# Three-layer graph convolution on one core: an opening whose edges come as one block a partition and are turned round by TensorE, and 16.5 instead of 15 chunks a dense block in layer 1

## The chip, the core and the metric

One core of a Trainium2 chip runs the whole program as one launch. The metric is the device time of one execution in microseconds (us); lower is better. TensorE (PE, with its weight loads as PEld), VectorE (DVE), ScalarE (ACT), GpSimd (POOL) and SyncE (SP) each run their own instructions in program order, and wait for each other by semaphores. DMAs are issued from the queues of SP, ACT and POOL.

## The reference, cut to what matters

```python
# x: (6250, 256) f32; src, dst: 100000 edges, sorted by dst
# W1: (256, 512), W2: (512, 512), W3: (512, 256)
def _gcn_layer(h_in, W, b, src, dst, norm_edge, n_nodes):
    h = h_in @ W
    msg = h[src] * norm_edge[:, None]
    agg = jax.ops.segment_sum(msg, dst, num_segments=n_nodes)
    return agg + b
src = jnp.concatenate([edge_index[0], loops])
dst = jnp.concatenate([edge_index[1], loops])
deg = jax.ops.segment_sum(jnp.ones_like(dst, dtype=x.dtype), dst, num_segments=n)
dinv = jnp.where(deg > 0, jax.lax.rsqrt(deg), 0.0)
norm_edge = dinv[src] * dinv[dst]
h = x
for W, b in ((W1, b1), (W2, b2), (W3, b3)):
    h = jax.nn.relu(_gcn_layer(h, W, b, src, dst, norm_edge, n))
# the kernel's result: _layernorm(x + h, axis=-1)
```

## The kernel before, in words

The 6250 nodes are cut into NB = 50 blocks of Q = 125 nodes; five groups of GRP = 10 blocks share an opening stage. Because the edges are sorted by their target, a block's edges are one run. Of each run the first CAP = 2048 edges are held as KF = 16 chunks of 128, and what lies behind them goes to a shared "rest" of each group. A layer sums neighbours in one of two ways. For a **gathered** block, each chunk is one indirect DMA from GpSimd (line 1260) that fetches 128 rows of a table in device memory, and one or two matmuls with a 0/1 matrix of the targets (line 1290) that add them into the block's 125 rows. For a **dense** block, the count matrix of the block against all 6250 nodes (`counts`, comparisons at line 603, matmuls at 678, copies at 637) is multiplied with all rows held on chip (`parts`): 50 matmuls of 512 columns (line 1362). In layer 1 the first FEW = 22 blocks are dense and the other 28 gathered; both kinds run interleaved, chunk by chunk, in an order written out by the Python loop in `layer`.

How many dense products a chunk gets stands in three lines, `first` being 10 and `spacing` 15 in layer 1 (called with i = 0), `done` the products so far and `begun` 0:

```python
until = min(len(dense) * NB, begun + int((chunk + 1 - first) * NB / spacing))
if i == 0:
    until = min(until, done + 3)
```

The part ahead of layer 1 is called the opening here. `tile_gnn_resnorm_kernel` first finds where each block's run begins (`at`, `line`, and `starts` for the DMA registers). Then `sorted_path` does this, in an order written out by hand:

- `load_edges` issues one DMA a block, 50 in all: 128 partitions with 16 edges each, that is runs of 128 bytes. SP issues 25 of them, ACT 15 and GpSimd 10 (line 712). They fill `ed`.
- `load_x` brings the rows of x for each group, two DMAs a group (`by_rows` cuts 125 rows into 112 and 13). Groups 0 and 1 are issued by GpSimd at the very start, groups 2, 3 and 4 by GpSimd behind its edges. `rows_of(room, g)` places groups 0 to 3 in the four quarters of `room`; group 4 has `last_x`.
- `counted(g)` has three stages for each group. The first takes the targets relative to the block (`dlo`, `near`, lines 779 and 782), and has TensorE and ScalarE find where they rise (784, 786, 788, 791). The second counts the degrees (796 to 806), in group 0 after `rest_counted`. The third takes 1/sqrt (808), scales the group's ten blocks of x in place (ACT at line 814, from group 2 on every second block on DVE at line 812) and stores them to the table `tab` in two halves of five blocks (line 79 of `by_rows`, on SP). In step k of the loop stand stage one of group k, stage three of group k-2 and stage two of group k-1.
- `upper(g)` (ACT, 822) and `lower(g)` (DVE, 826) split the scaled rows into the two halves of `parts`.
- `searches` finds the runs that the count matrices are made from (503 to 563), `matrices` makes these, two sub-matrices a step. Before, three of its steps stand in step k = 5 of the loop and two in k = 6.

The first gather of layer 1 waits for the last store to `tab`. `both_stored` then stores `parts` to a second table, five blocks at a time, from chunk 2 on every 5 chunks; `other_parts` splits group 3 in the first chunks.

## Time and profile before

| | |
|---|---|
| median of 3 runs | 2048.05 us (2047.35 to 2074.66) |
| profiled execution, its own time | 2061.76 us |
| span in its profile, first to last instruction | 2060.0 us |
| mean granted TensorE clock | 0.98 |
| PE / PEld busy | 1930.2 us (94%) / 1508.0 us (73%) |
| DVE / ACT / POOL busy | 1538.2 / 1330.5 / 1436.8 us |

The rows come from one profiled execution. Times in a row are microseconds from the start of its span unless marked ns; a row of a timeline is `start, duration, engine, line, operation, out<-in, count, [idle before <- what ended it]`. An engine name with a q behind it (SPq, ACTq) is the queue that issues DMAs.

### The profile page before, as it was taken

Reading aid. Unit: us, or ns where it says so; the run is one execution under the profiler, and the core shown is the slowest. Engines: PE = TensorE matmul, PEld = TensorE weight load, DVE = VectorE, ACT = ScalarE, POOL = GpSimd, SP = SyncE. Lnnn points to the kernel's source line nnn. Section 1 sums busy time; section 2 is a strip of 40 time slices with the busy share of each in tenths; the row PEclk is TensorE's granted clock in tenths of the full one; section 3 lists DMA queues with packets and bytes.
Section 4 is the critical chain, followed back from the end, with each engine's and each line's share of the span. In section 5 each row is a group of like instructions: output and inputs, shape, how many; then the busy total and the mean of one; then the engine's idle time right before and its main releaser. Section 6 shows DMA issues by size and latency. Waiting matters only on the chain.

```text
span 2060.0 us, 30151 instructions
## 1 busy us (share of the span) xinstructions
PE 1930.2 (94%) x8561; PEld 1508.0 (73%) x8561; DVE 1538.2 (75%) x2881; ACT 1330.5 (65%) x2525; POOL 1436.8 (70%) x1436
## 2 busy tenths in 40 slices
PE   4499999999997989999999999999999899999997
PEld 3377777777774657888777778888878778787785
DVE  5866787778776658877677886689778477777777
ACT  3566777677775657766567766677756565665553
POOL 4366766766767577777777777677776577777773
PEclk9999999999998999999999999999999999999998
DMA  8796989999999798998599988989989467777772
GB/s 174 256 289 187 253 242 248 250 255 253 259 246 323 208 290 255 276 285 267 171 270 276 265 235 261 278 262 260 271 251 252 118 182 189 187 187 193 180 190 81
DMA packets 228116, 482.83 MB, mean 234 GB/s; under 512 B 45117, under 2 KB 83583, under 8 KB 227940
## 3 DMA queue, kind: packets, MB, share of 16 engines
q0 software_dynamic: 123136, 315.59, 55.5%
q1 hardware_dynamic: 102500, 164.99, 28.0%
q8 instruction: 69, 1.13, 0.2%
q14 instruction: 107, 0.88, 0.1%
q10 hardware_dynamic: 2304, 0.25, 0.1%
HBM read 412.41 MB, written 68.25 MB: 233 GB/s over the span
## 4 chain that ended last, share of the span: by engine, by line
PE 74%; DMA 13%; issue 5%; POOL 3%; DVE 3%; ACT 1%; SPq 1%; POOLq 0%; ACTq 0%; DVEq 0%
PE sacc L1290 16%; PE smm L1362 7%; PE sacc L1362 7%; PE win_ps L1362 6%; PE mat_ps L1362 6%; DMA room<-tab,ssrc 6%; PE win_ps L1499 5%; DMA parts<-tab,ssrc 2%; PE win_ps L1519 2%; PE str L1362 2%; PE near_cols L1030 2%; PE str L1499 2%; PE sacc L1030 2%; PE mat_ps L1030 2%; PE smm L1030 2%
## 5 line engine op out<-in xcount | busy, mean ns | idle before, releaser
L1260 POOL DMA_INDIRECT room<-tab,ssrc x714 | 732.3, 1026 | 239.4 <-issue 105.5
L1290 PE MATMUL sacc<-halves,shot 128*125 128x512 f32 (+1 forms) x1596 | 558.8, 412 | 23.4 <-DVE halves L1326 6.8
L1326 DVE TENSOR_TENSOR halves<-room,halves 128x256 fp32r<-128x256 f32 (+1 forms) x641 | 339.8, 543 | 155.9 <-ACT halves L1322 147.6
L1260 POOL DMA_INDIRECT halves<-both,ssrc x352 | 333.8, 948 | 144.3 <-issue 35.7
L1322 ACT CAST halves<-room 128x256 fp32r<-128x256 f32 (+1 forms) x641 | 306.2, 501 | 153.9 <-DMA room<-tab,ssrc 116.6
L1198 ACT CAST piece<-room 125x625 fp32r<-125x625 uint8 x423 | 299.5, 716 | 126.8 <-PE mat_ps L1362 42.7
L1290 PEld LDWEIGHTS sacc<-halves,shot 128*125 128x125 f32 x1596 | 294.6, 189 | 116.0 <-DVE halves L1326 20.4
L603 DVE TENSOR_TENSOR room<-near_cols,slots 128x625 bf16<-128x625 f32 (+2 forms) x387 | 293.1, 804 | 56.3 <-PE sacc L678 22.5
L1260 POOL DMA_INDIRECT parts<-tab,ssrc x246 | 270.5, 1099 | 83.9 <-issue 50.6
L1362 PE MATMUL sacc<-parts,piece 125*125 125x512 f32 x600 | 192.9, 428 | 0.4 <-ACT piece L1198 0.4
L1362 PE MATMUL smm<-parts,piece 125*125 125x512 f32 x655 | 187.0, 405 | 0.6 <-DVE piece L1198 0.6
L1326 DVE TENSOR_TENSOR halves<-parts,halves 128x512 fp32r<-128x512 f32 x185 | 126.1, 695 | 53.0 <-ACT halves L1322 49.7
L1362 PE MATMUL win_ps<-parts,piece 125*125 125x512 f32 x550 | 152.3, 403 | 4.8 <-ACT piece L1198 4.8
L1362 PE MATMUL mat_ps<-parts,piece 125*125 125x512 f32 x550 | 150.1, 397 | 0.0
L678 PEld LDWEIGHTS <-room 128*125 128x125 bf16 x650 | 90.2, 141 | 71.8 <-issue 34.1
L1185 DVE TENSOR_TENSOR shot<-near_cols,sdlo 128x500 fp32r<-128x500 f32 x191 | 128.2, 671 | 18.9 <-PE sacc L1290 13.9
L1322 ACT CAST halves<-parts 128x512 fp32r<-128x512 f32 x185 | 111.8, 620 | 45.3 <-DMA parts<-tab,ssrc 17.4
L1362 PEld LDWEIGHTS smm<-parts,piece 125*125 125x125 f32 x655 | 117.8, 186 | 30.0 <-issue 3.5
L1499 PE MATMUL win_ps<-room,w_sb 128*128 128x250 f32 x512 | 123.6, 385 | 10.4 <-ACT room L1478 9.6
L1362 PEld LDWEIGHTS win_ps<-parts,piece 125*125 125x125 f32 x550 | 102.8, 190 | 30.5 <-ACT piece L1198 5.2
L976 DVE TENSOR_TENSOR parts<-parts 125x512 fp32r<-125x512 f32 x150 | 103.7, 692 | 25.3 <-ACT parts L974 24.0
L1499 PEld LDWEIGHTS win_ps<-room,w_sb 128*128 128x128 f32 x512 | 98.9, 195 | 28.4 <-ACT room L1478 12.4
(349 smaller groups left out, 3606.8 us busy)
## 6 DMA issues: line engine op xcount, KB each, us to landing
parts<-tab SPq DMA_DIRECT2D x166, 224.0 KB
kept<-room SPq DMA_DIRECT2D x30, 683.6 KB
room<-kept SPq DMA_DIRECT2D x30, 683.6 KB
tab<-st SPq DMA_DIRECT2D x74, 224.0 KB
room<-tab,ssrc POOLq DMA_INDIRECT x714
both<-parts SPq DMA_DIRECT2D x10, 1120.0 KB
own_row<-tab SPq DMA_DIRECT2D x38, 224.0 KB
parts<-kept SPq DMA_DIRECT2D x60, 136.7 KB
```

What stands on the lines that cost most here:

```text
L603: nc.vector.tensor_tensor(out, (keys if near_taken else near_cols)[:, :shape[2]].unsqueeze(1).to_broadcast(shape), numbers.unsqueeze(2).to ...
L678: nc.tensor.matmul(bank[:Q, len(pair) * 256:][:, :G * NB], lhsT=hot_lo, rhs=hot_key, start=True, stop=True)
L976: nc.vector.tensor_sub(to[:, HID:], row, to[:, :HID].bitcast(F32))
L1030: nc.tensor.matmul(team_banks[n][:, :TEAM * Q], lhsT=both_parts[u % 3][:, h * HID + n * P:h * HID + (n + 1) * P], rhs=team_pieces[u // PIE ...
L1185: nc.vector.tensor_tensor(hot[:, :n], (cols if near_taken else near_cols)[:, :Q].unsqueeze(1).to_broadcast([P, n, Q]), dlo.rearrange("p b ...
L1198: convert(piece, made_or_read[:, c * PIECE:(c + 1) * PIECE, :])
L1260: nc.gpsimd.indirect_dma_start(out=row, out_offset=None, in_=table, in_offset=bass.IndirectOffsetOnAxis(ap=at, axis=0))
L1290: nc.tensor.matmul(acc[:Q, :size], lhsT=hot, rhs=row[:, c0:c0 + size], start=(not own_product and k == c0 == 0), stop=(k == KF and c0 + si ...
L1322: nc.scalar.copy(halves[:, :width], landed[chunk - hi_lag])
L1326: nc.vector.tensor_sub(halves[:, width:], row, halves[:, :width].bitcast(F32))
L1362: nc.tensor.matmul(acc_d[:Q], lhsT=got[done // PIECE][:, k % PIECE, :], rhs=parts[:, k], start=(k == 0), stop=(k == NB - 1))
L1499: nc.tensor.matmul(h_ps[:, f, :], lhsT=w2_sb[:, k, (f2 + f) * P:(f2 + f + 1) * P], rhs=zt[:, k, :], start=(k == 0), stop=(k == KH - 1))
```

## The change

The 50 edge DMAs, `ed` and `starts` go. In their place GpSimd issues two indirect DMAs as soon as `at` is known: each of 50 partitions gets one block's 2048 edges, in two halves of 8 KB, in the quarters of `room` that groups 2 and 3 will use later. In the new `turned_round`, DVE subtracts the block's base and writes the targets as bf16 (`raised`), 16 matmuls with an identity turn them into [128 edges, block] in PSUM, DVE clips them into `near_all`, and ACT writes `dlo` from it; 16 transposes do the same for the sources (`src`). `counted` takes `near_all` and loses its first two DVE operations. x of groups 0 and 1 is loaded by SP at the start, of group 4 by ACT at the start of `sorted_path`, of groups 2 and 3 by SP once `turned_round` no longer needs their quarters. Group 2 is scaled by ACT alone. The splits run in the order 0, 1, 2, 4 (before: 1, 2, 0, 4) with four of `matrices`' steps in k = 6, and `spacing` becomes 16.5.

```diff
+SLOTS = (1, 2, 0, 3)
...
-    at = g // 10 * 2560 % room.shape[1]
+    at = SLOTS[g // 10] * 2560
...
+        near_all = dp1.tile([P, KF, NB], BF16, name="near_all")
+        same_b = dp1.tile([P, P], BF16, name="same_b")
+        turns = []
+        raised = dp1.tile([NB, KF, P], BF16, name="raised")
+        linear = [half.rearrange("b (p j t) -> b t j p", j=KF, t=2) for half in by_block]
+        sources = [words.rearrange("b (j p) -> b j p", p=P)
+                   for words in (w1_sb[:NB].rearrange("b k n -> b (k n)"), raised.rearrange("b j p -> b (j p)").bitcast(F32))]
+        FIT = 512 // NB
...
+        def turned_round():
+
+            banks = [common.pop() for _ in range(2)]
+            runs = [(bank, slice(j, min(KF, j + FIT))) for bank, j in zip(banks, range(0, KF, FIT))]
+            views = [(bank[:, :(js.stop - js.start) * NB].rearrange("p (j b) -> p j b", b=NB), js) for bank, js in runs]
+            at = [(j, bank[:, n * NB:(n + 1) * NB]) for bank, js in runs for n, j in enumerate(range(KF)[js])]
+            sides = [slice(0, P // 2), slice(P // 2, P)]
+            for half, side in zip(linear, sides):
+                nc.vector.tensor_scalar(raised[:, :, side], half[:, 1], less, None, op0=ALU.add)
+            for half, side in zip(linear, sides):
+                nc.scalar.copy(sources[0][:, :, side], half[:, 0, :KF // 2])
+            for j, to in at:
+                nc.tensor.matmul(to, lhsT=raised[:, j], rhs=same_b[:NB, :NB], start=True, stop=True)
+            for view, js in views:
+                nc.vector.tensor_single_scalar(near_all[:, js], view, float(Q + 1), op=ALU.min)
+            for half, side in zip(linear, sides):
+                nc.scalar.copy(sources[1][:, :, side], half[:, 0, KF // 2:])
+            for g in (2 * GRP, 3 * GRP):
+                load_x(nc.sync, x_of(g), g)
+            yield
+            for view, js in views:
+                nc.scalar.activation(dlo[:, :, js].rearrange("p b j -> p j b"), view, AF.Copy, bias=-1.0)
+            yield
+            for j, to in at:
+                nc.tensor.transpose(to, sources[j // (KF // 2)][:, j % (KF // 2)], same[:NB, :NB])
+            yield
+            for view, js in views:
+                nc.vector.tensor_copy(src[:, :, js].rearrange("p b j -> p j b"), view)
+            common.extend(reversed(banks))
+            yield
+
         def counted(g):
             gs = slice(g, g + GRP)
-            nc.vector.tensor_tensor(dlo[:, gs, :KF], ed[:, gs, :, 1],
-                                    base_i[:, gs].unsqueeze(2).to_broadcast([P, GRP, KF]), op=ALU.subtract)
-            near = dp.tile([P, KF, GRP], BF16, name="near")
-            nc.vector.tensor_scalar(near.rearrange("p j b -> p b j"), dlo[:, gs, :KF], float(Q), 1.0, op0=ALU.min, op1=ALU.add)
+            near = near_all[:, :, gs]
...
-                if g >= 2 * GRP and b % 2:
+                if g >= 3 * GRP and b % 2:
...
-            for g in range(0, 3 * GRP, GRP):
-                load_edges((SP, nc.sync, range(g, g + h)), (ACT, nc.scalar, range(g + h, g + GRP)))
-            for g in range(3 * GRP, NB, GRP):
-                load_edges((SP, nc.sync, range(g, g + h)))
+            load_x(nc.scalar, x_of(NB - GRP), NB - GRP)
...
-            for g in range(3 * GRP, NB, GRP):
-                load_edges((POOL, nc.gpsimd, range(g + h, g + GRP)))
-            for g in range(2 * GRP, NB, GRP):
-                load_x(nc.gpsimd, x_of(g), g)
...
+            turning = turned_round()
+            next(turning)
+            later = {0: (turning, searches, searches), 3: (searches, searches, (upper, 0)),
+                     4: (searches, turning, (lower, 0), (upper, GRP)),
+                     5: (searches, searches, turning, (lower, GRP), matrices, matrices, matrices),
+                     6: ((upper, 2 * GRP), matrices, matrices, (lower, 2 * GRP), (upper, NB - GRP), matrices, matrices, (lower, NB - GRP))}
...
-                if k == NG - 1:
-                    nc.vector.tensor_copy(src, ed[:, :, :, 0])
...
-    spacing = 15.0
+    spacing = 16.5
...
+            for g in range(0, 2 * GRP, GRP):
+                load_x(nc.sync, rows_of(room, g), g)
...
-            for g in range(0, 2 * GRP, GRP):
-                load_x(nc.gpsimd, rows_of(room, g), g)
...
+            nc.vector.tensor_scalar(less, own[:NB], -1.0, 1.0, op0=ALU.mult, op1=ALU.add)
...
+            nc.vector.tensor_scalar(begin[:, 0:1], at[:NB, 0:1], 0.0, float(P * EC), op0=ALU.max, op1=ALU.min)
+            nc.vector.tensor_single_scalar(begin[:, 1:2], begin[:, 0:1], CAP // 2, op=ALU.add)
+            for h in range(2):
+                nc.gpsimd.indirect_dma_start(
+                    out=by_block[h], out_offset=None, in_=edges,
+                    in_offset=bass.IndirectOffsetOnAxis(ap=begin[:, h:h + 1], axis=0))
```

## Rows read from the trace of the kernel before

**Rows 1.** The page: busy time of each engine, share of the span, instructions.

```profile
PE 1930.2 (94%) x8561; PEld 1508.0 (73%) x8561; DVE 1538.2 (75%) x2881; ACT 1330.5 (65%) x2525; POOL 1436.8 (70%) x1436
```

**Rows 2.** Stretches of 20 us: PE, PEld, DVE, ACT, POOL busy; PE clock, DMA, GB/s.

```profile
100.00:120.00 20.00, 20.00 (x99) 16.31 (x100) 14.71 (x23) 15.43 (x27) 12.71 (x14) 0.96 0.85 275
...
600.00:620.00 20.00, 20.00 (x98) 14.60 (x97) 16.65 (x27) 13.67 (x25) 14.28 (x16) 1.00 0.98 271
620.00:640.00 20.00, 12.80 (x58) 7.30 (x56) 18.82 (x31) 13.05 (x24) 14.82 (x16) 1.00 1.33 317
```

**Rows 3.** The same stretches, line 1362 (dense products) alone: PE, PEld busy.

```profile
620.00:640.00 20.00, 0.00 (x0) 0.00 (x0) 1.00 1.33 317
```

**Rows 4.** The chain that ended last, 0 to 170 us: start, duration, what.

```profile
0.88 3.08 DMA d_i<-in_dst
...
34.85 14.30 DMA ed<-in_edges
...
70.08 3.85 DMA b_sb<-in_L_gnn_b
...
87.53 11.62 DMA halves<-tab,ssrc
...
103.60 0.69 PE sacc L1362 x3
...
158.75 0.66 PE mat_ps L522 x2
```

**Rows 5.** Stretches of 4 us of the opening, columns as in rows 2.

```profile
12.00:16.00 4.00, 0.00 (x0) 0.00 (x0) 2.81 (x16) 0.00 (x0) 2.36 (x11) 1.00 1.03 221
...
20.00:24.00 4.00, 0.24 (x2) 0.05 (x2) 2.37 (x9) 0.00 (x0) 3.39 (x4) 1.00 0.39 42
```

**Rows 6.** Timeline of DVE, 0 to 105 us.

```profile
16.57 0.81 DVE L844 CAST nodes_up<-keys_i 128x1260 bf16<-128x1260 int32 x1
...
49.47 0.33 DVE L779 TENSOR_TENSOR sdlo<-ed,base_i 128x160 f32<-128x160 int32 x1 [7.07 <-DMA last_x<-in_x]
...
51.36 1.41 DVE L812 TENSOR_SCALAR room<-room,sdinv 125x256 f32<-125x256 f32 x5
...
61.90 3.79 DVE L603 TENSOR_TENSOR room<-near_cols,slots 128x625 bf16<-128x625 f32 x5
65.61 0.21 DVE L808 RECIPROCAL sdinv<-sroot 125x10 f32<-125x10 f32 x1
...
70.50 2.81 DVE L826 TENSOR_TENSOR parts<-last_x,parts 125x2560 fp32r<-125x2560 f32 x1
...
97.22 1.66 DVE L603 TENSOR_TENSOR room<-near_cols,slots 128x625 bf16<-128x625 f32 x2 [6.54 <-PE smm L678]
```

**Rows 7.** Timeline of ACT, 0 to 105 us.

```profile
28.53 0.29 ACT L786 CAST rises<-deg_bank 128x160 bf16<-128x160 f32 x1 [19.46 <-DMA ed<-in_edges]
...
36.35 4.10 ACT L814 ACTIVATE room<-room,sdinv 125x256 f32<-125x256 f32 x10 [0.31 <-DVE sdinv L808]
...
45.21 2.32 ACT L822 CAST parts<-room 125x2560 fp32r<-125x2560 f32 x1
```

**Rows 8.** Timeline of PE, 0 to 110 us.

```profile
16.54 1.64 PE L522 MATMUL win_ps<-d,w_sb 128*125 128x391 f32 x2 [5.83 <-DVE w_sb L509]
...
28.87 2.14 PE L791 MATMUL part_ps<-rises,begun 128*126 128x17 bf16 x10 [4.71 <-DVE begun L788]
...
38.97 0.45 PE L560 MATMUL sacc<-ident_r,w_sb 125*128 125x125 f32 x1
39.21 0.41 PE L561 MATMUL sacc<-ident_r,w_sb 125*128 125x125 f32 x1
```

**Rows 9.** Timeline of POOL, 0 to 100 us.

```profile
74.30 1.03 POOL L1260 DMA_INDIRECT halves<-tab,ssrc  x1 [38.83 <-DMA b_sb<-in_L_gnn_b]
```

**Rows 10.** Timeline of SP's queue, 0 to 100 us.

```profile
13.68 21.51 SPq L712 DMA_DIRECT2D ed<-in_edges  x25
...
67.18 2.85 SPq L79 DMA_DIRECT2D tab<-last_x  x4
```

More of the change, by code (lines that the diff above doesn't have):

```diff
@@ L392, in general_path, with sorted_path @@
         nc.scalar.dma_start(out=out[b * P:b * P + n, :], in_=o[:n])
+SLOTS = (1, 2, 0, 3)
 def rows_of(room, g):
-    at = g // 10 * 2560 % room.shape[1]
+    at = SLOTS[g // 10] * 2560
     return room[:Q, at:at + 2560].rearrange("p (b c) -> p b c", b=10)
 @with_exitstack
-def sorted_path(ctx: ExitStack, tc: tile.TileContext, x, edges, starts, found, wts, biases, room, late, out):
+def sorted_path(ctx: ExitStack, tc: tile.TileContext, x, edges, by_block, found, wts, biases, room, late, out):
     nc = tc.nc
@@ L420, in sorted_path @@
     d, nxt, ones, line, more, ends = found
+    by_block, less = by_block
     load_x, late_w, load_w2, load_w3 = late
@@ L697, in sorted_path @@
         deg_bank = psd1.tile([P, 512], F32, name="deg_bank")
-        ed = dp1.tile([P, NB, KF, 2], I32, name="ed")
         last_x = dp1.tile([P, GRP * C], F32, name="last_x")[:Q].rearrange("p (b c) -> p b c", b=GRP)
-        def load_edges(*loads):
-            todo = []
-            for eng, queue, blocks in loads:
-                _, places = nc.values_load_multi_w_load_instructions(
-                    starts[0:1, blocks[0]:blocks[-1] + 1], engines=[eng], min_val=0, max_val=edges.shape[0] - CAP,
-                    skip_runtime_bounds_check_because="a count of edges, behind which CAP more places are filled")
-                todo.append([(queue, b, at) for b, at in zip(blocks, places)])
-            for in_turn in zip(*todo):
-                for queue, b, at in in_turn:
-                    with nc.allow_non_contiguous_dma(reason="a run of edges over the partitions"):
-                        queue.dma_start(out=ed[:, b], in_=edges[ds(at, CAP), :].rearrange("(p j) t -> p j t", p=P))
         def x_of(g):
@@ L829, in sorted_path @@
             numbers()
-            h = GRP // 2
-            for g in range(0, 3 * GRP, GRP):
-                load_edges((SP, nc.sync, range(g, g + h)), (ACT, nc.scalar, range(g + h, g + GRP)))
-            for g in range(3 * GRP, NB, GRP):
-                load_edges((SP, nc.sync, range(g, g + h)))
+            load_x(nc.scalar, x_of(NB - GRP), NB - GRP)
             for table in (*tables, both_halves):
@@ L839, in sorted_path @@
             nc.vector.tensor_copy(own0, own_i)
+            nc.vector.tensor_copy(same_b, same)
             next(searches)
@@ L858, in sorted_path @@
                         next(stages[g])
-                for part, g in zip(splits.get(k, ())[::2], splits.get(k, ())[1::2]):
-                    if k == NG + 1 and g:
-                        next(matrices)
-                    part(g)
-                if k == 0:
-                    nc.vector.tensor_copy(ident_r, same)
-                    nc.vector.tensor_copy(loops, same)
+                if k == 1:
                     nc.vector.tensor_copy(keys, keys_i)
                     nc.vector.tensor_copy(near_cols, keys)
-                if k > 0 and seen == 0:
-                    next(searches)
-                    next(searches)
-                if k == NG - 1:
-                    nc.vector.tensor_copy(src, ed[:, :, :, 0])
-                if k == NG:
-                    assert seen == 1
-                    for _ in range(3):
-                        next(matrices)
+                for part in later.get(k, ()):
+                    if isinstance(part, tuple):
+                        part[0](part[1])
+                    else:
+                        next(part)
+            assert seen == 1
             late_w()
@@ L1678 @@
     ones = wpool.tile([P, 1], F32, name="fones")
-    starts = wpool.tile([1, NT], I32, name="starts")
+    by_block = [rows_of(room, g)[:NB].rearrange("b k c -> b (k c)")[:, :CAP].bitcast(I32) for g in (2 * GRP, 3 * GRP)]
+    begin = wpool.tile([NB, 2], I32, name="begin")
+    less = wpool.tile([NB, 1], F32, name="less")
     other = wpool.tile([1, 1], I32, name="other")
@@ L1770 @@
             nc.tensor.matmul(bad_ps, lhsT=bad, rhs=ones, start=True, stop=True)
-            nc.vector.tensor_copy(starts, line_ps[0:1, :])
             nc.vector.tensor_copy(line, line_ps)
@@ L1785 @@
     with tc.If(n_other == 0) as cmp:
-        sorted_path(tc, x, edges, starts, (d, nxt, ones, line, more, ends), (w1_sb, w2_sb, w3_sb), (b1, b2_sb, b3),
+        sorted_path(tc, x, edges, (by_block, less), (d, nxt, ones, line, more, ends), (w1_sb, w2_sb, w3_sb), (b1, b2_sb, b3),
                     room, (load_x, late_w, load_w2, load_w3), out)
```

6 lines of the change are left out of this document (2 added, 4 removed).

## The prediction, made before the changed kernel ran

> **What bounds the kernel now.** I read the page first: PE is busy for 94% of the span [rows 1]. A share over the whole span hides stages, so the stretches of 20 us came next. From 100 us on PE is full, and it stays so up to 620 us; then it has gaps, 7.2 us in the 20 us behind that [rows 2]. The dense products alone end at 620 us [rows 3]: layer 1 is bound by PE while its dense products last, and by the gathers behind them. Ahead of 100 us PE has little to do. There the chain of waits says what counts: a wait for edges that ends at 49.2 us, the last stores of the table, and then the rows of the first gathers [rows 4]. The timelines of the engines show the same from their side. DVE stands idle for 7.1 us until group 4's edges and x are there, at 49.47 [rows 6]; ACT's first copy waits until 28.53, because ACT has edge DMAs to issue before it [rows 7]; SP issues its 25 for 21.5 us [rows 10]. GpSimd waits for 38.8 us and gathers from 74.30 on [rows 9]. So a faster opening moves everything behind it forward by what the first gather and the first dense product gain; it cannot shorten the stretch in which PE is full.
>
> **The spacing.** The change from 15 to 16.5 chunks a block costs and gives nothing, and this needs no price. In layer 1 the number of products in a chunk is the smaller of the paced number and three. The paced number grows by 50/16.5 = 3.03 a chunk after the change and by 3.33 before. With chunk 10 the start, both are at least 3 times the chunks gone, so "done + 3" is the smaller one in every chunk, and the two kernels issue the same list. The chain shows the cap at work: L1362 comes three at a time [rows 4].
>
> **The edges.** Removed: 50 DMAs, 21.5 us of SP's queue [rows 10] and ACT's issuing ahead of 28.53 [rows 7]. While they run, the DMA queues carry 42 GB/s at a share of 0.39 [rows 5], which is what runs of 128 bytes give. Added: two gathers on GpSimd, issued when the run begins are known. That is some 3 us ahead of SP's first edge DMA at 13.68 [rows 10], as the branch and the last DVE steps of the finding lie between: issue starts near 10.5, and at 1.03 us each with a pause [rows 9] ends near 13. For 0.8 MB in rows of 8 KB there is no row. The low bound is the load of `d`, 0.4 MB in 3.1 us from issue to use [rows 4], so 14.6 for issue from 11.5; the high bound is a gather amid other transfers, 11.6 us [rows 4], so 23.1. Loads of x keep the DMAs full from 12 to 16 us [rows 5], so I take 17, nearer to the low end because the rows are long. This price is hidden: DVE has its small preparations until 17.4 before [rows 6], and with step, identity and bf16 copies moved ahead of the turning until about 18.5. Any landing up to 18.5 costs nothing; each us beyond is lost.
>
> **The turning.** On DVE two operations of 1024 elements on 50 partitions: at the rate of the cast of 1260 in 0.81 us [rows 6] they take 0.7 each, at that of the old `dlo` (160 in 0.33, [rows 6]) 2.1. I take 1.2 each, as the read is strided: until 21.0. On PE 16 small matmuls: ten of similar size took 2.14 in the opening [rows 8], 0.21 each, so 3.4, until 24.5. DVE's clip of the last six chunks (300 elements, at the compare's 3.79/5 for 625 [rows 6]) adds 0.4. ACT then copies half of the sources twice, 512 elements each: 0.5 by the rate of `upper` [rows 7], 0.9 by that of the copy of 160 in 0.29 [rows 7], say 0.7, until 26.1. So group 0's first ACT copy falls at 26.1 and not 28.53, 2.4 us earlier; the edges of all groups are there by then, but group 0 had nearly the same start before.
>
> One price hangs on TensorE's clock. The same pair of search products took 1.64 us at 16.5 [rows 8] and 0.66 at 158.8 [rows 4], while the granted clock reads 1.00, the level of 2.4 GHz, in both opening stretches shown [rows 5]. I therefore price PE's work in the opening by rows of the opening. The Trainium skill (TensorE: Matmul & The Clock Gate, section The HAM clock gate) says that the array's clock is throttled by default and is released by activity; the two durations agree with it, the clock column of the opening doesn't. At the durations of the later pair the turning and the transposes would be shorter by some 1.7 us on the path, and the gain below 6 us.
>
> **From there to the last store.** The steps between that copy and the first scaling are as before, where they took 28.53 to 36.35, 7.8 us [rows 7]; scaling of group 0 then starts at 33.8. Now ACT has no idle time. Its list up to the root of group 3 is three scalings of 4.1 [rows 7], one `upper` of 2.3 [rows 7], and seven copies and roots of 0.2 to 0.3: 16 us, so 49.8. Group 2's even scaling by ACT alone costs 2 us there and frees 1.4 on DVE [rows 6]. x of groups 2 and 3 leaves SP at 26 and must be there at 45; nothing of SP's is queued behind it but the stores, which start at 35. Then DVE sets the pace. Before, it had 16.1 us of work without a gap between 49.47 and the reciprocal of group 4 at 65.61 [rows 6]: two `lower` of 2.8, five compares of 3.8, two scalings of 1.4, which is 12.2, and 3.9 of small steps. After, from 49.8: one `lower`, five compares and one scaling, 8.0, and some 3 of small steps, among them a search step that now stands here and the copy of the sources. That copy needs the 16 transposes; two in a row started 0.24 us apart and took up to 0.45 [rows 8], so 3.8 to 7.2, I take 4.2, begun at 49.1 and so done at 53.3 when DVE gets there. The reciprocal comes at 49.8 + 8.0 + 3 + 0.4 = 61.2, **4.4 us earlier**. What follows it up to the first gather is the same: 65.61 to 74.30 before [rows 6, 9], so the first gather starts at 69.9. With 17 and 1.2 at their bounds (23.1; 0.7 to 2.1), and transposes at 7.2, the gain lies between -5 and +6 us.
>
> **Up to the dense products.** `lower` of groups 2 and 4 now both stand behind that reciprocal, and one stood there before, ending at 73.3 [rows 6]. DVE so ends the opening at about 72.7, but with two more steps of `matrices` done, three compares or 2.3 us: a lead of 3 us, and one search step deferred, together near 4. The first count matrix then comes 4 us earlier, and two chunks earlier in the order. Its last compares waited for PE until 97.22 [rows 6] behind gathered rows that were late; the rows come 4.4 us earlier too. I take 5 us for the start of the full stretch, which carries to the end as it is. POOL is relieved of the x loads and ten edge DMAs, which lay in a wait of 38.8 us [rows 9] and give nothing more.
>
> **The sum.** The profiled execution took 2061.8 us (span 2060.0 and 1.8 around it); less 5 gives 2056.8. It lies 13.7 above the median of the runs, so the same 5 off 2048.05 gives 2043. A change under 2%, 41 us, can't be told from none by a measurement at this bound.
>
> **The rivals.**
> - *Wait moved.* The first gathers start early, but their rows share the DMAs with the stores of `parts`, as the wait of 11.6 us shows [rows 4]. These stores follow `other_parts` on DVE, which gains only 3 to 4 us; if rows that now are early only meet the same stores, the full stretch starts within 2 us of before: 2047. For it: DVE waited 6.5 us for PE at this place [rows 6]. Against it: stores and rows move together. Chance 0.15.
> - *More than the sum.* The first six or seven gathers land ahead of those stores, the matrix is two chunks ahead, and PE fills from 88 to 90: 10 to 12 us, and up to 20 if the opening's small steps are cheaper too: 2036. Against it: rows 8 to 12 still meet the stores. Chance 0.18.
> - *Slower: edges late.* The two gathers share the DMA engines with 3.8 MB of x. From a landing at 23 the gain at the reciprocal is gone, as the slack ends at 18.5 and the gain is 4.4; at 30, near twice the high bound's delay, the kernel is 7 slower: 2055. For it: edge waits of 14.3 us were had in the old opening [rows 4]. Against it: those were many short runs behind x on one queue. Chance 0.12. The Trainium skill (DMA: Bandwidth & Descriptors, section Why a DMA increments its semaphore by 16 and not by 1) speaks against 50 partitions: a transfer takes the largest number of engines up to 16 that divides its rows, which is 10. No transfer here shows it. By the page's 27 GiB/s an engine, an estimate, both halves would take 2.8 us and not 1.8, which alone stays inside the slack.
> - *The spacing acts.* Were the cap not to hold, 33 chunks more for the same products would move work from the full stretch into gaps like the 7.2 us behind 620 [rows 2]; two such stretches give 15 us more: 2028. The cap's arithmetic speaks against it. Chance 0.02.
>
> **How the numbers follow.** The forecast, 2 to 9 us less, has 0.53, at 2043. The range takes in the rival of more, down to 2027, and the late edges up to 2056; outside are parts of both, together some 0.1. A change of 41 us either way needs something that none of these has: faster by over 2% 0.02, slower by over 2% 0.03, within 2% 0.95.
>
> **What would show it.** Right: the first DVE operation of the turning starts at 18 to 19, not on a DMA wait; ACT's first rise copy near 26; reciprocal of group 4 near 61; first gather near 70; PE full from about 95, with three products a chunk as before and the end of the dense products about 5 us earlier, and no other stretch changed. Wrong: a DVE wait on edges past 20; ACT not gapless from 34 to 50; DVE waiting for the transposes past 55; the first gather early but PE full from 100 as before; or a number of dense products in a chunk other than three.

## The result and the profile after

The changed kernel took 2042.14 us, the median of 11 runs (2036.19 to 2053.92); beside it the kernel before took 2053.17 (2047.35 to 2074.66, 11 runs). The ratio is 0.9948 [0.9924, 0.9972], 10.7 us less. That is within 2%, in the range, and twice the 5 us that were forecast. The same program was timed twice more (below): 0.9978 [0.9949, 1.0006] and 0.9964 [0.9933, 0.9995]. The mean of the three ratios is 0.9963, 7.6 us, so the first comparison lies at the large end of what repetition gives; the three intervals overlap. The profiled execution took 2037.44 us, its span 2035.7.

The page after, busy time and share of each engine, against [rows 1]:

```profile
PE 1917.3 (94%) x8593; PEld 1505.3 (74%) x8593; DVE 1531.0 (75%) x2874; ACT 1335.1 (66%) x2536; POOL 1401.9 (69%) x1418
```

PE is as full as before. The opening tells more. DVE's timeline after, with its wait in brackets (against [rows 6]):

```profile
23.24 1.16 DVE L783 TENSOR_SCALAR raised<-room,less 50x1024 bf16<-50x1024 int32 x1 [6.00 <-DMA room<-in_edges,begin]
27.22 1.17 DVE L783 TENSOR_SCALAR raised<-room,less 50x1024 bf16<-50x1024 int32 x1 [2.82 <-DMA room<-in_edges,begin]
...
33.23 0.23 DVE L764 TENSOR_TENSOR sdlo<-rest,base_i 128x50 f32<-128x50 int32 x1
...
37.48 0.21 DVE L834 RECIPROCAL sdinv<-sroot 125x10 f32<-125x10 f32 x1
...
53.12 0.21 DVE L834 RECIPROCAL sdinv<-sroot 125x10 f32<-125x10 f32 x1 [1.43 <-ACT sroot L832]
...
64.15 0.21 DVE L834 RECIPROCAL sdinv<-sroot 125x10 f32<-125x10 f32 x1
```

The edges arrive at 23.24 and 27.22, not at 17. The three reciprocals are those of groups 0, 3 and 4; the last came at 65.61 before [rows 6], so in this profile the opening's long list of steps ends 1.5 us earlier, where 4.4 were forecast. In the two other profiles of this program (below) it ends at 60.27 and 63.15, 5.3 and 2.5 us earlier, because the edges land earlier there: in all three it comes 36.9 us behind the landing of the second half (27.22, 23.32 and 26.21). PE's timeline after (against [rows 8]):

```profile
28.45 0.85 PE L787 MATMUL sacc<-same_b,raised 50*128 50x50 bf16 x16 [8.94 <-DVE raised L783]
...
52.17 1.09 PE L799 MATMUL sacc<-same,w 50*128 50x50 f32 x8
...
53.07 1.05 PE L799 MATMUL sacc<-same,raised 50*128 50x50 f32 x8
...
93.61 0.97 PE L1376 MATMUL sacc<-parts,piece 125*125 125x512 f32 x3 [0.65 <-ACT piece L1212]
```

The 16 turning matmuls take 0.85 us in all, the 16 transposes 2.1 (the two rows added); the first dense product starts at 93.61. Before, it started at 99.91, and PE had waited for gathered rows until 91.69 and 95.54:

```profile
91.69 1.21 PE L1290 MATMUL sacc<-halves,shot 128*125 128x256 f32 x2 [3.95 <-DMA halves<-tab,ssrc]
...
95.54 1.22 PE L1290 MATMUL sacc<-halves,shot 128*125 128x256 f32 x2 [2.23 <-DMA halves<-tab,ssrc]
...
99.91 1.65 PE L1362 MATMUL sacc<-parts,piece 125*125 125x512 f32 x3 [0.39 <-ACT piece L1198]
```

ACT's timeline after (against [rows 7]): copies, a scaling of ten rows, and the root of group 3.

```profile
29.29 2.04 ACT L791 CAST raised<-room 50x512 f32<-50x512 int32 x2 [0.91 <-PE sacc L787]
...
37.73 4.10 ACT L840 ACTIVATE room<-room,sdinv 125x256 f32<-125x256 f32 x10
...
52.92 0.17 ACT L832 ACTIVATE sroot<-deg_bank 125x10 f32<-125x10 f32 x1
```

POOL's timeline after: the two gathers of edges, the first gather of layer 1 (74.30 before, [rows 9]), and the first gathers of layers 2 and 3.

```profile
9.92 1.11 POOL L1785 DMA_INDIRECT room<-in_edges,begin  x1 [8.06 <-DVE begin L1783]
...
11.33 0.94 POOL L1785 DMA_INDIRECT room<-in_edges,begin  x1 [0.31 <-DVE more L1798]
...
72.74 0.96 POOL L1274 DMA_INDIRECT halves<-tab,ssrc  x1 [38.32 <-DMA both<-parts]
...
714.27 0.95 POOL L1274 DMA_INDIRECT room<-tab,rest  x1 [17.24 <-DMA tab<-st]
...
1590.75 0.95 POOL L1274 DMA_INDIRECT room<-tab,rest  x1 [27.89 <-DMA tab<-st]
```

And the last two of these in the kernel before:

```profile
723.05 0.95 POOL L1260 DMA_INDIRECT room<-tab,rest  x1 [15.35 <-DMA parts<-tab]
...
1613.70 0.94 POOL L1260 DMA_INDIRECT room<-tab,rest  x1 [25.39 <-DMA tab<-st]
```

Layer 2 so starts 8.8 us earlier. From there to layer 3's first gather it is 876.5 us after and 890.7 before, and from layer 3's first gather to the end 444.9 and 446.3. The two spans differ by 24.3 us, which is more than the runs' 8 to 11; the 14 us inside layer 2 are looked at with the repeated program below.

The chain of waits after, where the dense products begin (start, duration, what; against [rows 4]):

```profile
92.57 0.21 DVE room L633
...
102.06 12.88 DMA halves<-tab,ssrc
114.99 0.70 PE sacc L1304 x2
...
115.90 0.70 PE sacc L1376 x3
...
117.26 0.69 PE sacc L1376 x3
```

The first count matrix, finished by DVE at 92.57, sets the start at 93.61. Gathered rows that arrive late (12.88 us in this chain, 11.62 before [rows 4]) still hold PE behind it: it waits 1.48 us for them up to 106.42 and 0.92 up to 114.99. Behind them a chunk's products, three of them dense, repeat every 1.36 us (115.90 to 117.26).

### The profile page after: what moved, and what is told of

Its sections match the earlier page's. It is cut to its first block, busy times and chain, and to the rows that moved or that the text cites. A ratio compares the mean times of both kernels' runs of the same rounds, so it can differ in the third digit from the quotient of the medians.

```text
span 2035.7 us, 30025 instructions
## 1 busy us (share of the span) xinstructions
PE 1917.3 (94%) x8593; PEld 1505.3 (74%) x8593; DVE 1531.0 (75%) x2874; ACT 1335.1 (66%) x2536; POOL 1401.9 (69%) x1418
## 3 DMA queue, kind: packets, MB, share of 16 engines
q1 hardware_dynamic: 104016, 169.70, 29.6%
## 4 chain that ended last, share of the span: by engine, by line
PE 73%; DMA 12%; issue 4%; DVE 3%; POOL 3%; ACT 1%; SPq 0%; ACTq 0%; POOLq 0%; DVEq 0%
PE sacc L1304 15%; PE sacc L1376 8%; PE smm L1376 7%; PE mat_ps L1376 7%; PE win_ps L1376 6%; DMA room<-tab,ssrc 6%; PE win_ps L1513 4%; DMA parts<-tab,ssrc 3%; PE win_ps L1533 2%; POOL room L1274 2%; PE smm L1044 2%; PE near_cols L1044 2%; PE sacc L1044 2%; PE mat_ps L1044 2%; DMA halves<-both,ssrc 2%
## 5 line engine op out<-in xcount | busy, mean ns | idle before, releaser
L1274 POOL DMA_INDIRECT room<-tab,ssrc x714 | 723.6, 1013 | 245.7 <-issue 118.9
L1304 PE MATMUL sacc<-halves,shot 128*125 128x512 f32 (+1 forms) x1562 | 543.5, 411 | 20.7 <-ACT halves L1336 8.2
L1304 PEld LDWEIGHTS sacc<-halves,shot 128*125 128x125 f32 x1562 | 287.9, 189 | 103.2 <-DVE halves L1340 16.6
L1274 POOL DMA_INDIRECT parts<-tab,ssrc x246 | 254.1, 1033 | 83.8 <-issue 52.1
L1376 PE MATMUL sacc<-parts,piece 125*125 125x512 f32 x700 | 222.5, 425 | 0.6 <-ACT piece L1212 0.6
L1376 PE MATMUL smm<-parts,piece 125*125 125x512 f32 x605 | 170.3, 402 | 0.8 <-DVE piece L1212 0.8
L1376 PE MATMUL mat_ps<-parts,piece 125*125 125x512 f32 x600 | 167.0, 400 | 0.0
L641 ACT CAST room<-sacc 125x500 uint8<-125x500 f32 (+1 forms) x142 | 98.3, 696 | 61.0 <-PE sacc L682 60.0
L1376 PEld LDWEIGHTS sacc<-parts,piece 125*125 125x125 f32 x700 | 114.6, 187 | 24.3 <-issue 7.8
L1376 PEld LDWEIGHTS smm<-parts,piece 125*125 125x125 f32 x605 | 109.5, 186 | 27.2 <-issue 1.5
L1376 PEld LDWEIGHTS mat_ps<-parts,piece 125*125 125x125 f32 x600 | 109.6, 186 | 26.2 <-issue 1.0
```

The source lines that it names most:

```text
L641: nc.scalar.copy(place[:, :, u * G:(u + len(ms)) * G].rearrange("p k (t r) -> p t k r", r=G), counted_in.rearrange("p (t v) -> p t v", t=2 ...
L1274: nc.gpsimd.indirect_dma_start(out=row, out_offset=None, in_=table, in_offset=bass.IndirectOffsetOnAxis(ap=at, axis=0))
L1304: nc.tensor.matmul(acc[:Q, :size], lhsT=hot, rhs=row[:, c0:c0 + size], start=(not own_product and k == c0 == 0), stop=(k == KF and c0 + si ...
L1376: nc.tensor.matmul(acc_d[:Q], lhsT=got[done // PIECE][:, k % PIECE, :], rhs=parts[:, k], start=(k == 0), stop=(k == NB - 1))
```

## The experiments

All kernels compute the whole reference. They ran on three chips, each time beside the kernel before. On one of these it took 2336 us, so whole times are compared across chips only as ratios.

**Is the spacing inert?** The changed kernel with the old spacing:

```diff
-    spacing = 16.5
+    spacing = 15.0
```

> The changed kernel with spacing 15 instead of 16.5. Theory (the cap of three products a chunk makes spacing idle): the same time as the changed kernel, 0.993 to 0.997 of the kernel before, last dense product of layer 1 near 608 us in its profile. Rival (the spacing acts): half the gain or more is gone, 0.997 to 1.002, last dense product 5 us or more away from 608. The profile also gives a second look at layer 2 (723 to 1614 us before, 714 to 1591 after): if its 14 us less belongs to the change, this profile has about 877 us there again; if it varies from execution to execution, anything from 870 to 895.

Measured: 2044.91 us, ratio 0.9978 [0.9949, 1.0006]. The instruction lists of all engines are identical to those of the changed kernel, so this is the same program once more, and its distance from the 0.9948 is what repetition gives. Its reciprocal of group 4 on DVE, its first dense product on PE and its first gathers of layers 2 and 3 on POOL:

```profile
60.27 0.22 DVE L834 RECIPROCAL sdinv<-sroot 125x10 f32<-125x10 f32 x1
```

```profile
90.02 0.97 PE L1376 MATMUL sacc<-parts,piece 125*125 125x512 f32 x3 [1.55 <-ACT piece L1212]
```

```profile
714.09 0.94 POOL L1274 DMA_INDIRECT room<-tab,rest  x1 [19.93 <-DMA tab<-st]
...
1592.94 0.94 POOL L1274 DMA_INDIRECT room<-tab,rest  x1 [26.91 <-DMA tab<-st]
```

**Edges or matrix steps?** The opening after also does two more steps of `matrices` ahead of the gathers. One kernel takes them from the change, the other gives them to the kernel before:

```diff
-                     6: ((upper, 2 * GRP), matrices, matrices, (lower, 2 * GRP), (upper, NB - GRP), matrices, matrices, (lower, NB - GRP))}
+                     6: ((upper, 2 * GRP), matrices, (lower, 2 * GRP), (upper, NB - GRP), matrices, (lower, NB - GRP))}
```

> The changed kernel with five steps of the count matrices in the opening, as before, instead of seven. Theory (of the 6.3 us by which the first dense product came earlier, 1.6 come from the reciprocal of group 4 and the rest from the two more steps): first gather at 71 to 73 us, first dense product at 96 to 98, ratio to before 0.996 to 0.999. Rival (the edges and the turning made it all): first dense product within 1 us of 93.6, ratio 0.993 to 0.997.

```diff
                     if k == NG + 1 and g:
                         next(matrices)
+                        next(matrices)
```

> The kernel before with two more steps of the count matrices in step 6 of its opening, so seven. Theory (steps and edges each give a part): first gather as before (74 to 76), first dense product at 95 to 98 instead of 99.9, ratio 0.996 to 0.999. Rival (the steps are the whole gain): first dense product at 94 or earlier, ratio 0.993 to 0.996. Rival (the steps only move DVE work): 99 to 101, ratio 0.999 to 1.002.

Measured: 2044.1 us, 0.9954 [0.9936, 0.9971], for the edges without the steps, and 2051.86, 0.9991 [0.9968, 1.0014], for the steps without the edges. DVE's reciprocal of group 4, PE's last wait for gathered rows and its first dense product, and POOL's first gather of layer 2, with the edges only:

```profile
63.18 0.20 DVE L834 RECIPROCAL sdinv<-sroot 125x10 f32<-125x10 f32 x1
```

```profile
95.49 1.22 PE L1304 MATMUL sacc<-halves,shot 128*125 128x256 f32 x2 [2.35 <-DMA halves<-tab,ssrc]
...
99.91 1.64 PE L1376 MATMUL smm<-parts,piece 125*125 125x512 f32 x3 [1.10 <-ACT piece L1212]
```

```profile
717.03 0.94 POOL L1274 DMA_INDIRECT room<-tab,rest  x1 [15.51 <-DMA parts<-tab]
```

and with the steps only:

```profile
93.55 1.64 PE L1363 MATMUL str<-parts,piece 125*125 125x512 f32 x3
```

```profile
720.10 0.94 POOL L1261 DMA_INDIRECT room<-tab,rest  x1 [17.88 <-DMA parts<-tab]
```

Without the steps the first dense product stands at 99.91, as before, though the reciprocal of group 4 came 2.4 us and the first gather 2.6 us earlier (63.18, 71.72): PE waits for gathered rows until 95.49, where before it waited until 95.54. With the steps alone the start is 93.55, about as after. So the steps are needed for the earlier start. Once they are there the edges count too: in the three profiles of the changed program the first dense product comes 29.5, 29.8 and 29.6 us behind the reciprocal of group 4 (64.15 and 93.61; 60.27 and 90.02; 63.15 and 92.73, below), so it starts as much earlier as the edges let the opening end.

This start is not yet the lead at layer 2: there the edges alone are 6.0 us ahead of before, the steps alone 3.0, both 8.8. By 200 us PE has done 187 dense products before, 198 with either half, and 209, 219 and 209 in the three profiles of the changed program. These three differ by as much as a half brings, so single profiles can't divide the lead. Nor do the whole times: by means it is 8.8 us for the edges alone and none for the steps alone, with standard errors of 1.6 and 2.0, and the edges alone are not worse than the whole change. How the gain divides stays open.

**Would earlier edges have paid?** In the changed kernel the two gathers of edges share the DMA engines with loads of x. Here only x of group 0 starts ahead of them:

```diff
 (ahead of the search for the runs)
-            for g in range(0, 2 * GRP, GRP):
-                load_x(nc.sync, rows_of(room, g), g)
+            load_x(nc.sync, rows_of(room, 0), 0)
 (in sorted_path, behind numbers())
-            load_x(nc.scalar, x_of(NB - GRP), NB - GRP)
+            load_x(nc.sync, x_of(GRP), GRP)
 (in turned_round, behind ACT's first copies)
+            load_x(nc.scalar, x_of(NB - GRP), NB - GRP)
```

> The changed kernel with x of group 1 issued by SP only after the branch and x of group 4 by ACT behind its first copies of the sources, so that less stands in the DMA queues when the edges are gathered. Theory (the edges landed at 23 and 27 us because 3.8 MB of x shared the engines with them): the second turning operation of DVE starts at 17 to 20 instead of 27.2, the reciprocal of group 4 comes at 56 to 60 instead of 64.2, first gather 66 to 70, first dense product 87 to 92, ratio 0.989 to 0.994. Rival (50 rows of 8 KB take that long by themselves): second turning operation still at 25 to 28 and the ratio that of the changed kernel. Rival (earlier opening, but the first rows wait for the stores of the parts): reciprocal at 60 or earlier, first dense product still 92 to 95, ratio 0.993 to 0.997.

Measured: 2050.02 us, 0.9988 [0.9966, 1.0011]. DVE's timeline in it:

```profile
17.27 1.19 DVE L783 TENSOR_SCALAR raised<-room,less 50x1024 bf16<-50x1024 int32 x1
19.61 1.17 DVE L783 TENSOR_SCALAR raised<-room,less 50x1024 bf16<-50x1024 int32 x1 [1.15 <-DMA room<-in_edges,begin]
...
30.06 0.24 DVE L764 TENSOR_TENSOR sdlo<-rest,base_i 128x50 f32<-128x50 int32 x1 [4.36 <-DMA rest<-in_edges,place_i]
```

The first half of the edges is there by 17.27, as forecast, the second at 19.61, but now the five small `rest` gathers are late: DVE stands for them until 30.06. The reciprocal of group 4 comes at 61.00, within the 60.27 to 64.15 that three profiles of the unchanged program show. The same with all of x behind the edges:

```diff
 (ahead of the search for the runs)
-            for g in range(0, 2 * GRP, GRP):
-                load_x(nc.sync, rows_of(room, g), g)
 (in sorted_path, behind numbers())
-            load_x(nc.scalar, x_of(NB - GRP), NB - GRP)
 (in turned_round, behind ACT's first copies)
+            for g in range(0, 2 * GRP, GRP):
+                load_x(nc.scalar, x_of(g), g)
 (in turned_round, behind ACT's second copies)
-            for g in (2 * GRP, 3 * GRP):
+            for g in (2 * GRP, 3 * GRP, NB - GRP):
                 load_x(nc.sync, x_of(g), g)
```

> The changed kernel with all loads of x issued only behind the gathers of the edges (groups 0 and 1 by ACT behind its first copies of the sources, 2, 3 and 4 by SP), a look at the landing of the edges alone. Theory (the 3.8 MB of x were what held them back): both turning operations of DVE start without a DMA wait of over 1 us, at 17 to 19 us; x of group 0 then comes late and the first scaling starts after 36 us, so the time is that of before or worse. Rival (50 rows of 8 KB are slow by themselves): the second operation at 22 us or later.

A single run took 2323.96 us, against 2336 of before on that chip; one run gives no ratio. DVE's timeline in it:

```profile
17.29 2.48 DVE L783 TENSOR_SCALAR raised<-room,less 50x1024 bf16<-50x1024 int32 x2
...
30.06 0.24 DVE L764 TENSOR_TENSOR sdlo<-rest,base_i 128x50 f32<-128x50 int32 x1 [5.31 <-DMA rest<-in_edges,place_i]
```

Now neither operation waits: the first half is there by 17.29, the second by 18.60, where the second operation starts. The wait for `rest` ends at the same 30.06, so the wait is moved, not removed. In the traces the last packet of `rest` ends at 27.5 us in the changed kernel, and at 28.6 and 28.8 in these two, while loads of x keep the DMA engines at shares of 1.10 to 1.21 from 22 to 30 us; the edges, as long as they came later, hid that. An order in which DVE needs `rest` later was not tried. The first kernel of this pair took 5 us more than the changed program on its chip (2050.02 and 2044.91), and nothing in its layer 1 explains that. It was run again beside the changed kernel:

> The kernel with x of group 1 behind the branch and of group 4 behind the first copies, a second time, with the changed kernel on the same chip. Its first gather of layer 2 came 2 us earlier than the changed kernel's, and yet 12 runs took 5.9 us more (two standard errors are 4.4). Theory (chance, no mechanism in sight: the instruction lists behind the opening are the same): within 4 us of the changed kernel, and DVE waits for the rest gathers until 29 to 31 us again, so that no gain is left of the earlier edges. Rival (the order of the loads does something lasting): 4 us or more slower than the changed kernel again.

Measured: 2045.84 us, 0.9982 [0.995, 1.0014], beside 2044.18 for the changed kernel. The 5 us did not come back, and earlier edges show no gain that can be measured.

**The changed kernel once more**, unaltered, on the third chip:

> The changed kernel itself, for a third profile of it and as the measure for the three beside it. Theory (the first gather of layer 2 comes 9 us earlier through the change; how long layer 2 takes differs between executions of one program): ratio to before 0.993 to 0.998, and a length of layer 2 (first gather to that of layer 3) that differs by 5 us or more from one of the 876.5 and 878.9 us that its two profiles had on the first chip, or that tells nothing, if this is another chip. Rival (the shorter layer 2 belongs to the change): 875 to 880 again on such a chip.

Measured: 2044.18 us, 0.9964 [0.9933, 0.9995]. Its reciprocal of group 4, its first dense product and its first gathers of layers 2 and 3:

```profile
63.15 0.21 DVE L834 RECIPROCAL sdinv<-sroot 125x10 f32<-125x10 f32 x1
```

```profile
92.73 0.96 PE L1376 MATMUL sacc<-parts,piece 125*125 125x512 f32 x3 [1.62 <-ACT piece L1212]
```

```profile
713.38 0.94 POOL L1274 DMA_INDIRECT room<-tab,rest  x1 [16.84 <-DMA tab<-st]
...
1598.07 0.94 POOL L1274 DMA_INDIRECT room<-tab,rest  x1 [26.89 <-DMA tab<-st]
```

In three profiles of one program layer 2 starts at 713.4 to 714.3 and lasts 876.5, 878.9 and 884.7 us; with the edges first, where layer 1's work is the same, it lasts 894.0 and 897.3. The lead at layer 2's start is steady (8.8 to 9.7 us); what layer 2 adds is not. So the 14 us inside layer 2 between the profiles of before and after are mostly no part of the gain; whether a few of them are stays open, as the kernel before lies at 890.7 and 894.0 (with the steps).

**Where does the spacing begin to act?** Spacing 18.5, on two chips:

```diff
-    spacing = 16.5
+    spacing = 18.5
```

> The changed kernel with spacing 18.5, so 2.70 dense products a chunk, fewer than the cap of three. Theory (spacing acts only where it falls below the cap): products a chunk no longer three in each, the last dense product of layer 1 some 13 chunks further on in the order and so at 605 to 620 us, with more gathers done by then; the gaps of PE behind it (7.2 us in 20 us before) shrink, the first gather of layer 2 comes at 703 to 712 instead of 714, ratio to before 0.990 to 0.995. Rival (the end of layer 1 is bound by its own gathers and by the work of the teams, which starts when the last dense block is finished): first gather of layer 2 at 713 to 720, ratio 0.995 to 0.999.

> The changed kernel with spacing 18.5, now with the changed kernel on the same chip. Theory (2.70 products a chunk move PE's work into the gaps behind the dense products): 0.996 to 0.999 of the changed kernel's time, first gather of layer 2 0 to 6 us earlier than in it. Rival (the end of layer 1 is bound by gathers and teams): 0.999 to 1.003 of it.

Measured: 0.9887 [0.983, 0.9944] on the chip where before takes 2336, and 2027.26 us, 0.989 [0.9844, 0.9935], beside the 2044.18 of the changed kernel: 17 us less. The dense products alone (line 1376), first for the changed kernel run again, then for spacing 18.5:

```profile
400.00:600.00 200.00, 140.51 (x444) 72.98 (x443) 1.00 0.92 252
600.00:620.00 20.00, 4.24 (x13) 2.12 (x13) 0.91 1.23 305
```

```profile
400.00:600.00 200.00, 143.15 (x431) 70.68 (x430) 1.00 0.98 271
600.00:620.00 20.00, 14.43 (x45) 7.11 (x45) 1.00 0.99 271
```

and the first gather of layer 2 with spacing 18.5:

```profile
696.82 1.06 POOL L1274 DMA_INDIRECT room<-tab,rest  x1 [19.00 <-DMA parts<-tab]
```

With 148 gathers issued from 400 to 600 us in the one and 160 in the other, a chunk carries 3.0 dense products and then 2.7. Layer 2 starts at 696.82 and not 713.38, 16.6 us earlier, where at most 6 were expected. The expected reason, that PE's work moves into its gaps, does not show: from 100 us to layer 2's start PE is idle for 17.6 us in the changed kernel and for 19.4 here. What moves is the gathers: with fewer dense products in a chunk they follow each other faster, and layer 1's last one is issued at 676.88 instead of 695.23. The first gather of layer 2 follows the last one of layer 1 by 18 to 20 us in both. PE also begins products of layer 2 early, behind the last dense block (line 1044): 167 of them stand ahead of layer 2's first gather in the changed kernel and 98 here, and the rest runs inside layer 2, which lasts 885.1 us, no longer than in the changed kernel (884.7). So the rival was right that gathers bind the end of layer 1, and wrong that the spacing would not move them. The other way round, the cap raised, with the old spacing so that the paced number doesn't hold it:

```diff
-                    until = min(until, done + 3)
+                    until = min(until, done + 4)
...
-    spacing = 16.5
+    spacing = 15.0
```

> The changed kernel with a cap of four products a chunk instead of three and spacing 15, so that 3.33 a chunk are issued. Theory (the cap is what holds the pace): the last dense product of layer 1 comes 15 to 35 us earlier than 607, the gaps behind it grow by about as much, first gather of layer 2 within 5 us of 714, ratio 0.994 to 1.001. Rival (the pace is held by the count matrices, not by the cap): the last dense product within 5 us of 607 and the same time as the changed kernel.

Measured: 1.0019 [0.9989, 1.0049]. From 600 to 700 us 50 dense products are left, where spacing 18.5 on the same chip leaves 179, and layer 2 starts at 776.5 against 769.7: with more dense products in a chunk fewer gathers are issued before (132 against 137 from 400 to 600 us), and behind the products that end early PE stands idle (74.5 us busy of these 100 against 90.8).

**Group 2's even split**, given back to ACT and DVE together, alone and with spacing 18.5:

```diff
-                if g >= 3 * GRP and b % 2:
+                if g >= 2 * GRP and b % 2:
```

> The changed kernel with every second block of group 2 scaled by DVE again, as before. Theory (ACT's list sets the pace from the first scaling to the root of group 3): from the first reciprocal to the fourth 13.6 us instead of 15.6, the fifth about 2 us earlier against the first, ratio within 0.002 of the changed kernel's. Rival (DVE sets the pace there too): fourth reciprocal less than 1 us earlier against the first.

> The changed kernel with spacing 18.5 and with every second block of group 2 scaled by DVE. Theory (both help a little and add): 0.995 to 0.999 of the changed kernel's time, the fourth reciprocal 1.1 us earlier against the first (14.5 instead of 15.6). Rival (one of them takes the other's place): the time of the better one alone, within 2 us.

Measured: 0.9906 [0.9872, 0.994] alone, and 2024.2 us, 0.9873 [0.9829, 0.9918], with both; spacing 18.5 alone gave 0.989 on that chip, and the intervals overlap. DVE's reciprocals of groups 0, 3 and 4 in the first:

```profile
33.75 0.21 DVE L834 RECIPROCAL sdinv<-sroot 125x10 f32<-125x10 f32 x1
...
48.32 0.22 DVE L834 RECIPROCAL sdinv<-sroot 125x10 f32<-125x10 f32 x1
...
59.35 0.22 DVE L834 RECIPROCAL sdinv<-sroot 125x10 f32<-125x10 f32 x1
```

From group 0 to group 3 it is 14.57 us, 15.64 after (53.12 less 37.48): ACT's list is on the path, and the split is worth 1.07 there (14.54 in the kernel with both), half of the 2 us that the prediction put on ACT. The 22 us of that ratio can't all come from 1 us in the opening; of the changed kernel itself no ratio was taken on that chip, so how much of them is the split's stays open. The kernel with both is the fastest of the study, 27 us under before and 20 under the changed kernel on the same chip.

## Why the prediction was right or wrong

- **Spacing: right.** The instruction lists are the same, and the number begins to matter only where 50 chunks over the spacing fall below the cap of three. That 18.5 measures 2027 us, where the rival of an acting spacing had 2028, is luck: the rival meant 16.5 without the cap, and work that moves into gaps of PE, which the run with 18.5 doesn't show.
- **Edges landing at 17: wrong**, the step that failed first. They land at 23.24 and 27.22 (20.14 and 23.32, 22.45 and 26.21 in the two other profiles of the program), the second half past the high bound of 23.1. That bound counts from 11.5, ahead of the second gather's issue, which the forecast ended near 13; counted from there it is 24.6, and two of the three pass that too. I chose near the low end for the rows' length; without x on the engines that is nearly right (17.29 and 18.60 at the latest), with it not, and x was in the trace that I had. The opening follows the second half one for one, 36.9 us from it to group 4's reciprocal in all three profiles, until the edges land before some 20: at 19.61 `rest` is what DVE waits for. The Trainium skill (DMA: Bandwidth & Descriptors, section Why a DMA increments its semaphore by 16 and not by 1) would put 50 rows on 10 engines. The trace of the kernel with all of x behind the edges agrees: ten packets of 8 KB are in flight from 12.0 to 13.0 us, while the first gather runs alone, and 16 from 13.8 to 14.4, with the second beside it.
- **The slower rival's condition was met, its price not.** It had the gain gone from a landing at 23; in the three profiles 1.5, 5.3 and 2.5 us of the 4.4 at the reciprocal are there. The second half came 10.2 us later than forecast, and ACT's first scaling at 37.73 only 3.9 later than the 33.8. Of the difference 1.5 was slack, 1.2 was the first half's turning, done during the wait, 2.6 was PE (0.85 for 3.4), and the rest smaller steps behind (6.4 us from ACT's copies to the scaling, not 7.7), less slower copies (2.04 for the two).
- **PE's small operations: mis-sized** by four times in the turning (0.05 us each, forecast 0.21) and by two in the transposes (2.1 us, forecast 4.2). The rows that I took, ten products in 2.14 [rows 8], were no bound for sixteen back to back. The clock is not the reason: the sixteen took 0.85 us in a stretch with a granted clock of 0.50 and 0.84 in another profile in one of 1.00. DVE's 1.2 each was right (1.16).
- **ACT's and DVE's lists: right.** From the first scaling to the end of group 3's root it took 15.4 us (forecast 16), from there to group 4's reciprocal 11.1 (11.4; the 0.4 in that sum stood for nothing that I had named), and 8.6 from it to the first gather (8.7). Group 4's reciprocal is some 3 us later than the forecast 61.2 because the scaling began 3.9 later.
- **Dense products 5 us earlier: 6.3, 9.9 and 7.2 in the three profiles, nearly right in size, but half of its reason fell.** I had put it to two leads at once, the rows and the matrix. The lead of DVE on the matrix was not there: DVE ended its opening at 76.5 us, not at 72.7, 3 us later than before, and the two steps that it had done more are worth 2.2. I had also counted one `lower` behind group 4's reciprocal before, where there are two (67.17 and 70.50). What the steps bring is the place in the order: before, DVE's last compares waited 6.54 us for PE behind the late rows [rows 6]; after, DVE waits nowhere longer than 0.6 us from there on and finishes the matrix at 92.57. Then the lead of the opening counts in full.
- **"Carries to the end as it is": not so.** In the three profiles the lead over before is 6.3, 9.9 and 7.2 us at the first dense product, 8.7, 12.3 and 8.7 at the last (607.51, 603.99 and 607.55 against 616.24), and 8.8, 9.0 and 9.7 at layer 2's start. In the stretch that I took for full it grows by 1.5 to 2.4 us. For the first profile two parts of this can be read. PE's gap of 3.4 us from 120 to 140 before is gone after, but one of 2.4 from 100 to 120 has come, so 1.0 is gained. And before, the granted clock reads 0.50 (1.2 GHz) from 92 to 100 us, where PE had stood idle for 3.95 and 2.23 us, and the first chunk with dense products takes 2.1 us (99.91 to 102.01); after, it reads 1.00 (2.4 GHz) from 92 to 96, and that chunk takes 1.4. Behind the last dense product a lead of 12.3 is worth no more than one of 8.7: POOL then waits 19.93 us for the last stores to `tab`, and 17.24 and 16.84 in the other two. So the forecast missed a size: I took a full PE from 100 us on, and passed over the gap in it and the waits behind it.
- **The sum of 5 is near the 7.6 of the three comparisons in part by luck**: the edges brought less than 4.4 at the reciprocal in two profiles of three, the matrix nothing by DVE's lead, and the lead grew behind, which the sum didn't have. The rival "more than the sum" had its mechanism right (earlier rows, a matrix ahead) and with 10 to 12 us was as near.
- **"Wait moved" was right as a mechanism in two other kernels**: with the edges only, where gathers that start 2.6 us earlier meet rows that come no earlier (95.49 and 95.54; the stores of `parts` are issued at 81.14 and 81.82), and from edges to `rest`, once the edges are early. In the changed kernel the steps take the first dense product out of the first of these waits.

## What to carry to other kernels

A new early transfer is priced by what else is on the DMA engines at that time, and before it is hurried one looks at which transfer is last behind it. A lead is read where the next stage starts: here leads of 6.3 to 9.9 us at the start of a full stretch all came to some 9 at its end, since other waits bind there. A step that stands behind a late transfer in program order is worth moving ahead of it, even where it saves its engine no time. A pacing number beside a cap does nothing until the paced value falls below the cap; work out that point first, and try the values on its far side, since here they were worth more than the whole change.

## What was not expected of the hardware

- Two gathers of 50 rows of 8 KB, 0.8 MB in all, land some 12 and 15 us after their issue while x shares the engines (11.03 to 23.24, 12.27 to 27.22) and some 6 us at most each when it doesn't (11.09 to 17.29, 12.34 to 18.60). The small `rest` gathers, whose issue then ends at 22.4, are there only at 30.06: the DMA engines were at 0.19 from 18 to 20 us, but at 1.10 to 1.21 from 22 to 30, when the loads of x had come (read from the kernel with all of x behind the edges).
- The granted clock and the durations disagree in the opening. The same pair of search products in two executions of the changed program, each with its stretch (columns as in [rows 5]):

```profile
72.97 1.67 PE L526 MATMUL win_ps<-d,w_sb 128*125 128x391 f32 x2
```

```profile
72.00:76.00 4.00, 3.60 (x11) 2.18 (x10) 4.00 (x4) 4.00 (x7) 2.95 (x2) 0.50 0.95 326
```

```profile
69.09 1.67 PE L526 MATMUL win_ps<-d,w_sb 128*125 128x391 f32 x2
```

```profile
68.00:72.00 4.00, 3.48 (x11) 2.18 (x10) 4.00 (x4) 4.00 (x7) 2.84 (x2) 1.00 0.93 339
```

  The first stretch reads 0.50, the level of 1.2 GHz, the second 1.00, that of 2.4 GHz; the pair takes 1.67 us in both, and 0.82 at 158.59 in the kernel before, in the full stretch (the chain of waits counts 0.66 of it [rows 4]).
- One program's layer 2 lasted 876.5 to 884.7 us in three profiles, and on one chip the kernel before took 2336 us, where its medians beside the other runs were 2051 to 2053.
